# Splitting the contraction of a graph product into two 64-row halves that sum in two PSUM banks

## The chip, the cores and the metric

The kernel runs on one core of one Trainium2 chip. The metric is the device time of one execution in microseconds (us). Lower is better. I quote the median of several executions.

## The reference, cut to what matters

Four layers of graph operations act on x of shape (8, 2048, 64). Each of the first three multiplies by the same 2048 x 2048 matrix `adj`:

```python
h = relu(layernorm(x)); x = x + L0(h, adj, ...)   # T1 = A h, T2 = A T1, then weights per node
h = relu(layernorm(x)); x = x + L1(h, adj, ...)   # three steps: v = relu([v, A v] W1' + b1) W2' + b2
h = relu(layernorm(x)); x = x + L2(h, adj, ...)   # A h, a column scale, one small matmul
h = relu(layernorm(x)); x = x + L3(h, adj, ...)   # attention; with this adj a mean over the nodes
```

The matrix is 0/1 with every row scaled, so the kernel keeps its signs in `BT` (float32r, exact) and scales the result by a row of constants, `crow`. To hold precision, every operand is split into a rounded part H and a rest L, both float32r, and both are multiplied.

## The kernel before

Two of the eight batches go together as 128 feature columns. A product is 16 chunks of 128 nodes, each with H and L, so 32 matmuls of 128 rows and 512 columns, which all add into one PSUM bank. There are 88 calls of it: 24 in layer 0, 48 in layer 1 and 16 in layer 2. `fill` puts other work between chunks.

```python
def product(hl, nb, name, out, crow, fill={}):
    ps = bank("mm", f"bv_{name}")                       # one bank, two in rotation
    for m in range(NCH):                                # 16 chunks
        for i in range(2):                              # H, L
            nc.tensor.matmul(ps, hl[m // 4][i][:, m % 4, :], BT[:, m, nb * 512:(nb + 1) * 512],
                             start=(m == 0 and i == 0), stop=(m == NCH - 1 and i == 1))
        if m in fill:
            fill[m]()
    return scaled(ps, out, crow)                        # VectorE: out = ps * crow

def back_to_nodes(fT, wmat, name, tag="big"):           # "bn": four 128-row fp32 matmuls
    ps = psums[-1].tile([P, 4, 2 * C], F32, tag=tag, name=f"bn_{name}")
    ...

# layer 0, weights per node: y, 64-row fp32 matmuls, one half of the rows for each batch
y = psums[-1].tile([P, 2, 512], F32, tag="big", ...)    # a pair of banks, two pairs in rotation
for k in range(K):
    for bb in range(2):
        hs_ = slice(bb * C, (bb + 1) * C)
        nc.tensor.matmul(y[:, bb, :], terms[k][hs_, ts], wt[hs_, k, ...], ...)

# layer 1, one step of three (cut)
for nb in range(NB):
    ph = bank("tr", f"ph_{nm}")
    fill = {8: mid} if nb == 3 else {}                  # mid: bn of quarter 2
    fill[12] = lambda: nc.tensor.matmul(ph, w1v2 if s else w1vT, gT[nb], start=True, stop=True)
    product(hl, nb, nm, g, crow, fill=fill)
    gadd = nc.vector.tensor_tensor(g, ph, g, op=ALU.add)
    nc.scalar.activation(g, g, AF.Relu, bias=...)
    if nb in (1, 2):
        finish(nb - 1)                                  # bn of g, add, H and L for the next step
...
finish(3)
```

ph, bn, pt (transposes) and pS (sums over nodes) use all 128 rows. The order in which each engine runs its instructions is fixed when the program is built, and it need not be the order of this text.

Of the kernel before, what the change touches and what calls it, by code (L numbers as in the profile page):

```python
# [8 lines left out]
F32 = mybir.dt.float32  # L9
# [5 lines left out]
ALU = mybir.AluOpType  # L15
# [27 lines left out]
def uniform_path(  # L43
# [30 lines left out]
    nc = tc.nc  # L74
    P = 128
    B, N, C = x.shape
    NP = B // 2
    NCH = N // P
# [7 lines left out]
    psums = [pro.enter_context(tc.tile_pool(name="psump", bufs=1, space=bass.MemoryType.PSUM))]  # L86
# [5 lines left out]
    BT = adjp.tile([P, NCH, N], F32R, name="BT")  # L92
# [8 lines left out]
    def bank(tag, name):  # L101
        return psums[-1].tile([P, 512], F32, tag=tag, name=name)
# [12 lines left out]
    def part(nb):  # L115
        return slice(4 * nb, 4 * nb + 4)

    def load_x(layer, p, nb, queue=nc.sync):
        acc = block("acc", f"acc_{layer}_{p}_{nb}", 2)
        fill_x(acc, layer, p, nb, queue)  # L120
        return acc
# [12 lines left out]
    def load_h(p, nb, name, pool):  # L134
        t = pool.tile([P, 4, 2 * C], F32, tag="hb", name=f"hb_{name}", bufs=2)
        (nc.sync if lastp else nc.scalar).dma_start(t, hs[p][:, part(nb), :])
        return t

    def load_crow(nb, name, tag="crow"):
        t = work.tile([P, 512], F32, tag=tag, name=f"crow_{name}", bufs=2)  # L140
        nc.sync.dma_start(t, crowD[:, nb * 512:(nb + 1) * 512].to_broadcast([P, 512]))
        return t
# [41 lines left out]
    def go_on():  # L184

        with tc.issue_after(ahead.pop().ins) if ahead else nullcontext():
            for e in list(pending):
                next(e[0])
                e[1] -= 1
                if e[1] == 0:  # L190
                    pending.remove(e)
        ahead.clear()
# [8 lines left out]
    def halves(src, name, pool=None, later=None):  # L201

        pool, bufs = (work, 6) if pool is None else (pool, 4)
        Hq = pool.tile([P, 4, 2 * C], F32R, tag="H", name=f"H_{name}", bufs=bufs)
        Lq = pool.tile([P, 4, 2 * C], F32R, tag="L", name=f"L_{name}", bufs=bufs)
        copies.append(nc.scalar.copy(Hq, src))  # L206
        def rest():
            lows.append(nc.vector.tensor_tensor(Lq, src, Hq.bitcast(F32), op=ALU.subtract))

        rest() if later is None else later.append(rest)  # L210
        return Hq, Lq

    def scaled(ps, out, crow):
        ahead.append(nc.vector.tensor_tensor(out, ps, crow, op=ALU.mult))  # L214
        return out

    def product(hl, nb, name, out, crow, fill={}):

        ps = bank("mm", f"bv_{name}")
        for m in range(NCH):  # L220
            for i in range(2):
                nc.tensor.matmul(  # L222
                    ps, hl[m // 4][i][:, m % 4, :], BT[:, m, nb * 512:(nb + 1) * 512],
                    start=(m == 0 and i == 0), stop=(m == NCH - 1 and i == 1),
                )
            if m in fill:
                fill[m]()
        return scaled(ps, out, crow)

    def transposed(src, name):  # L230

# [5 lines left out]
    def to_feat(h, out, name):  # L237
        pt = transposed(lambda t: h[:, t, :], name)
        nc.scalar.copy(out, pt.rearrange("p t n -> p (t n)"))
        return out  # L240
# [41 lines left out]
    def spare(tag, name):  # L282
        return work.tile([P, 512], F32, tag=tag, name=name, bufs=6)
# [5 lines left out]
    dg = [spare("HL"[q % 2], f"dg_{q}").rearrange("p (j n) -> p j n", j=4) for q in range(NB)]  # L289
# [197 lines left out]
    nm = "0_1_3a"  # L487
    tx = work.tile([P, 512], F32, tag="z", name=f"t1T_{nm}", bufs=3)
    ps = bank("b1", f"bv_{nm}")
    for m in range(NCH):  # L490
        if m in (2, 7, 12):
            go_back(1 + m // 5)
        for i in range(2):
            nc.tensor.matmul(
                ps, hls[1][m // 4][i][:, m % 4, :], BT[:, m, 3 * 512:],
                start=(m == 0 and i == 0), stop=(m == NCH - 1 and i == 1),
# [77 lines left out]
    w1e = consts.tile([P, P], F32, name="w1e")  # L574
    ivt = consts.tile([1, P], F32, name="ivt")

    def feat(i, name):

        if i == 0:
            return term(1, name)  # L580
        return lastp[0].tile([P, 512], F32, tag="fm", name=name, bufs=4)

    def back_to_nodes(fT, wmat, name, tag="big"):

        ps = psums[-1].tile([P, 4, 2 * C], F32, tag=tag, name=f"bn_{name}")
        for t in range(4):
            nc.tensor.matmul(ps[:, t, :], fT[:, t * P:(t + 1) * P], wmat, start=True, stop=True)  # L587
        return ps
# [5 lines left out]
    def prepare_next(n, q):  # L594
        if n >= len(items):
            return
        layer, p = items[n]
        nm = f"{layer}_{p}_{q}"
        hl, gT = ops.setdefault(n, ([], []))
        h = load_h(p, q, nm, lastp[0] if n else l0q)  # L600
        if layer == 1:
            if q == 0:
                nc.scalar.copy(h[0:1, 0, :], ivt)
            gT.append(to_feat(h, feat(0, f"gT_{nm}"), nm))
            h = back_to_nodes(gT[q], w1e, f"u_{nm}", "big" if n else "mm")
        hl.append(halves(h, nm))

    def keep(p, nb, acc, name, more=None):

        norm_relu(acc, name, lambda z: nc.gpsimd.dma_start(hs[p][:, part(nb), :], z))  # L610
        if more is not None:
            nc.gpsimd.tensor_tensor(acc, acc, more, op=ALU.add)  # L612
        kept.append(nc.gpsimd.dma_start(xs[p][:, part(nb), :], acc))  # L613
# [3 lines left out]
    def node_weights(p, nb, terms, between=None):  # L617
        acc = load_x(0, p, nb)
        bn = l0q.tile([P, 4, C], F32, name="bn", bufs=2)
        nc.sync.dma_start(bn, biasD[:, part(nb), :])  # L620

        odd = l0q.tile([P, 4, 2 * C], F32, name="odd")
        av = acc.rearrange("p j (b c) -> p j b c", b=2)
        ov = odd.rearrange("p j (b c) -> p j b c", b=2)
        for t in range(4):
            ts = slice(t * P, (t + 1) * P)
            for dg in range(D // DG):
                y = psums[-1].tile([P, 2, 512], F32, tag="big", name=f"y_{p}_{nb}_{t}_{dg}")
                for k in range(K):
                    for bb in range(2):  # L630
                        hs_ = slice(bb * C, (bb + 1) * C)
                        nc.tensor.matmul(  # L632
                            y[:, bb, :], terms[k][hs_, ts], wt[hs_, k, dg * 512:(dg + 1) * 512],
                            start=(k == 0), stop=(k == K - 1),
                        )
                for d in range(DG):
                    e = dg * DG + d
                    yd, ec = y[:, :, d * C:(d + 1) * C], emb[:, 4 * nb + t, e:e + 1]
                    xj = (av, ov)[d % 2][:, t]
                    old = xj if e != 1 else bn[:, t, None, :].to_broadcast([P, 2, C])  # L640
                    last = nc.vector.scalar_tensor_tensor(  # L641
                        xj, yd, ec, old, op0=ALU.mult, op1=ALU.add
                    )
            ahead.append(last)
            chain.append(last)
            go_on()
            if between:
                between(t)
        nc.vector.tensor_tensor(acc, acc, odd, op=ALU.add)  # L649
        keep(p, nb, acc, f"1_{p}_{nb}")  # L650
# [6 lines left out]
    for p in range(NP):  # L657
# [27 lines left out]
        for nb in range(NB):  # L685
            nm = f"0_{p}_{nb}b"
            crow = load_crow(nb, nm)
            t2T = product(
                hl1, nb, nm, term(2, f"t2T_{nm}"), crow,
                fill={8: lambda: prepare(2)} if nb == 3  # L690
                else {12: lambda: first_t0.append(feat_0(0, 0))} if p + nb == 0 else {},
            )
            if p + nb == 0:
                t0T = first_t0[0]
            go_on()
            if nb == 3:
                prepare(3)
            t0T_next = feat_0(*divmod(4 * p + nb + 1, 4)) if 4 * p + nb + 1 < 4 * NP else None
            node_weights(
                p, nb, (t0T, t1T[nb], t2T),  # L700
                (lambda t: prepare_next(0, t)) if 4 * p + nb + 1 == 4 * NP else None,
            )
            t0T = t0T_next
            if nb in (1, 2):
                prepare(nb - 1)
            with tc.issue_after(kept[-1].ins):
                m = 4 * p + nb
                nc.gpsimd.dma_start(MD[m * P:(m + 1) * P, :], BTf[:, m, :])
            if p == 0:
                reload_t1(nb)  # L710
                norm_0(2, nb)
        if p == 0:
            hl1, t1T = hl_next, t1T_next
        else:
            hl = hl_next
# [56 lines left out]
    def layer1(n, p):  # L772
        hl, gT = ops[n]
        steps = 3
        for s in range(steps):
# [16 lines left out]
            def mid():  # L792
                if last:
                    prepare_next(n + 1, 2)
                else:
                    finish(2)
# [715 lines left out]
```

## Time and profile before

| before | value |
|---|---|
| time, median | 1279.28 us |
| span of the profiled execution | 1278.6 us |
| busy: TensorE, VectorE, ScalarE, GpSimd | 95%, 59%, 14%, 19% |
| first y to first ph (layer 0) | 553.5 us |
| first ph to first result of layer 2 (layer 1) | 458.0 us |
| from there to the end | 162.5 us |

TensorE is the bound. Its busy share says less than it seems to, since the recorded durations of pipelined matmuls overlap. In the views, PE is TensorE, PEld its weight loads, DVE VectorE, ACT ScalarE, POOL GpSimd and SP SyncE; L222 is line 222 of the kernel.

### The profile page before, as it was taken

To read this page: it belongs to the slowest core of one execution; us is meant where nothing else is said; L and a number is where in the kernel's file an instruction comes from. 1 tells how busy PE (TensorE), PEld (TensorE's weight loads), DVE (VectorE), ACT (ScalarE), POOL (GpSimd) and SP (SyncE) were. 2 spreads that over 40 slices of the span, in tenths; PEclk is the share of its full clock that TensorE was granted. 3 is DMA by queue.
4 is the path that set the end of the run, shared out by engine and by line. 5 is a ranking of instruction groups with operands and counts; after the bars stand their busy time and mean duration, and the time that the engine had idled before them with its cause. 6 is when DMAs were issued, how large, how long until landed. Compare 5 with 4: busy or idle time off the path is not lost.

```text
span 1278.6 us, 15515 instructions
## 1 busy us (share of the span) xinstructions
PE 1217.3 (95%) x5702; PEld 862.7 (67%) x5702; DVE 751.4 (59%) x1936; ACT 182.3 (14%) x281; POOL 236.8 (19%) x244
## 2 busy tenths in 40 slices
PE   4899999999999999999999999999999999999993
PEld 3665554555575556755567888787788787788882
DVE  5445887767746776377654446445543554575653
ACT  5530010000010000000011121112111111211100
POOL 6410211111121111011110024004102400432222
PEclk9999999999999999999999999999999999999996
DMA  8982343323332222122255425433643543524321
GB/s 265 343 208 74 96 112 87 90 70 84 95 105 71 71 79 66 65 62 62 67 141 136 102 93 158 112 92 121 150 117 87 159 116 86 161 95 115 108 58 36
DMA packets 140057, 141.14 MB, mean 110 GB/s; under 512 B 95093, under 2 KB 97141, under 8 KB 137925
## 3 DMA queue, kind: packets, MB, share of 16 engines
q1 hardware_dynamic: 121092, 82.05, 25.2%
q0 software_dynamic: 12160, 49.10, 12.8%
q10 hardware_dynamic: 6720, 8.92, 2.5%
q8 instruction: 47, 0.77, 0.2%
q14 instruction: 38, 0.30, 0.1%
HBM read 95.92 MB, written 35.73 MB: 103 GB/s over the span
## 4 chain that ended last, share of the span: by engine, by line
PE 83%; DMA 6%; DVE 4%; issue 3%; POOL 2%; ACT 1%; SPq 0%; ACTq 0%; POOLq 0%; DVEq 0%
PE bv L222 34%; PE y L632 23%; PE bn L587 4%; PE ph L804 3%; PE bv_0b L222 2%; PE bv_2b L222 2%; DMA BT<-in_adj_dram 2%; PE bv_3b L222 2%; PE bv_1b L222 2%; DMA hb<-hs 1%; POOL rstd L170 1%; PE bv_0a L222 1%; PE bv_3a L222 1%; PE bv_2a L222 1%; PE bv_1a L222 1%
## 5 line engine op out<-in xcount | busy, mean ns | idle before, releaser
L222 PE MATMUL bv<-BT,H 128*128 128x512 f32 x1024 | 426.7, 417 | 0.0
L222 PE MATMUL bv<-BT,L 128*128 128x512 f32 x1024 | 401.2, 392 | 0.0
L222 PEld LDWEIGHTS bv<-BT,H 128*128 128x128 f32 x1024 | 192.6, 188 | 47.9 <-issue 11.6
L222 PEld LDWEIGHTS bv<-BT,L 128*128 128x128 f32 x1024 | 192.9, 188 | 47.3 <-issue 11.5
L641 DVE SCALAR_TENSOR_TENSOR acc<-y,emb,acc 128x128 f32<-128x128 f32 x512 | 176.2, 344 | 65.8 <-PE y L632 62.4
L632 PE MATMUL y<-wt,t0T 64*128 64x512 f32 x512 | 144.2, 608 | 10.0 <-DVE odd L641 10.0
L641 DVE SCALAR_TENSOR_TENSOR odd<-y,emb,odd 128x128 f32<-128x128 f32 x448 | 153.3, 342 | 0.0
L170 POOL TENSOR_TENSOR rstd<-var,mhalf 128x8 f32<-128x8 f32 x64 | 107.9, 1688 | 194.5 <-DVE var L168 184.3
L214 DVE TENSOR_TENSOR g<-bv,crow 128x512 f32<-128x512 f32 x48 | 33.2, 691 | 183.7 <-PE bv L222 183.7
L164 ACT ACTIVATE sq<-z 128x512 f32<-128x512 f32 x64 | 40.4, 631 | 406.5 <-DVE z L160 397.4
L632 PEld LDWEIGHTS y<-wt,t0T 64*128 64x128 f32 x512 | 46.7, 187 | 73.9 <-issue 68.0
L612 POOL TENSOR_TENSOR acc<-acc,wl 128x512 f32<-128x512 f32 x16 | 20.6, 1289 | 297.3 <-DVE z L160 297.2
L613 POOL DMA_DIRECT2D xs<-acc x32 | 18.0, 562 | 276.2 <-DVE acc L649 254.2
L632 PE MATMUL y<-wt,t1T 64*128 64x512 f32 x256 | 67.9, 596 | 0.0
L173 DVE SCALAR_TENSOR_TENSOR z<-z,rstd 128x512 f32<-128x512 f32 x64 | 45.9, 723 | 28.2 <-POOL rstd L170 28.2
L587 PEld LDWEIGHTS bn<-wl,g 128*128 128x128 f32 x384 | 49.5, 191 | 6.3 <-ACT H L206 1.6
L167 DVE TENSOR_REDUCE var<-sq 128x8 f32<-128x512 f32 x64 | 43.5, 679 | 15.8 <-ACT sq L164 15.8
L587 PE MATMUL bn<-wl,g 128*128 128x128 f32 x384 | 51.1, 276 | 1.0 <-DVE var L168 0.5
L749 DVE SCALAR_TENSOR_TENSOR junk<-mt,cols,st 128x512 uint8<-128x512 bf16 x64 | 50.8, 794 | 0.6
L632 PEld LDWEIGHTS y<-wt,t1T 64*128 64x128 f32 x256 | 27.7, 188 | 27.3 <-issue 27.3
L809 ACT ACTIVATE g<-g,b1s 128x512 f32<-128x512 f32 x32 | 23.2, 724 | 139.4 <-DVE g L808 139.3
L160 DVE TENSOR_TENSOR z<-acc,mean 128x512 f32<-128x512 f32 x56 | 38.3, 690 | 6.6 <-DMA hs<-z 5.2
(209 smaller groups left out, 1677.3 us busy)
## 6 DMA issues: line engine op xcount, KB each, us to landing
BT<-in_adj_dram POOLq DMA_DIRECT2D x16, 1024.0 KB, 9.2
crow<-crowD SPq DMA_DIRECT2D x64, 256.0 KB, 3.2
st<-in_adj_dram SPq DMA_DIRECT2D x64, 256.0 KB, 3.4
hs<-z POOLq DMA_DIRECT2D x40, 256.0 KB, 2.8
xs<-acc POOLq DMA_DIRECT2D x32, 256.0 KB, 2.5
MD<-BT POOLq DMA_DIRECT2D x16, 512.0 KB, 5.0
acc<-xs SPq DMA_DIRECT2D x32, 256.0 KB, 3.2
hb<-hs SPq DMA_DIRECT2D x28, 256.0 KB, 3.6
```

The lines of the kernel that those rows point to most:

```text
L160: firsts.append(nc.vector.tensor_tensor(g, groups(xt), mean[:, :, None].to_broadcast([P, 8, C]), op=ALU.subtract))
L164: squares.append(nc.scalar.activation(sq, z, AF.Square))
L167: nc.vector.tensor_reduce(var, groups(sq), axis=AX.X, op=ALU.add)
L170: powers.append(nc.gpsimd.tensor_tensor(rstd, var, mhalf, op=ALU.pow))
L173: nc.vector.scalar_tensor_tensor(groups(h), g, 0.0, rstd[:, :, None].to_broadcast([P, 8, C]), op0=ALU.max, op1=ALU.mult)
L214: ahead.append(nc.vector.tensor_tensor(out, ps, crow, op=ALU.mult))
L222: nc.tensor.matmul(ps, hl[m // 4][i][:, m % 4, :], BT[:, m, nb * 512:(nb + 1) * 512], start=(m == 0 and i == 0), stop=(m == NCH - 1 and i ...
L587: nc.tensor.matmul(ps[:, t, :], fT[:, t * P:(t + 1) * P], wmat, start=True, stop=True)
L632: nc.tensor.matmul(y[:, bb, :], terms[k][hs_, ts], wt[hs_, k, dg * 512:(dg + 1) * 512], start=(k == 0), stop=(k == K - 1),)
L641: last = nc.vector.scalar_tensor_tensor(xj, yd, ec, old, op0=ALU.mult, op1=ALU.add)
L749: nc.vector.scalar_tensor_tensor(junk, mt, cols[:, i, :], st, op0=ALU.mult, op1=ALU.not_equal, accum_out=bad[:, i, q:q + 1],)
L804: fill[12] = lambda: nc.tensor.matmul(ph, w1v2 if s else w1vT, gT[nb], start=True, stop=True)
```

## The change

The intent is to let the two halves of the array work on the two halves of a chunk at the same time, so that the loading of weights for one half hides behind the other. Each half sums in a bank of its own, so a product now has two banks of sums, which ScalarE (a copy) and VectorE (an add) join. For the banks, y and the products share three pairs, and bn moves to the two "tr" banks.

```diff
     def product(hl, nb, name, out, crow, fill={}):
-        ps = bank("mm", f"bv_{name}")
+        ps = psums[-1].tile([P, 2, 512], F32, tag="big", name=f"bv_{name}", bufs=3)
         for m in range(NCH):
             for i in range(2):
-                nc.tensor.matmul(
-                    ps, hl[m // 4][i][:, m % 4, :], BT[:, m, nb * 512:(nb + 1) * 512],
-                    start=(m == 0 and i == 0), stop=(m == NCH - 1 and i == 1),
-                )
+                for r in range(2):
+                    rows = slice(r * C, (r + 1) * C)
+                    nc.tensor.matmul(
+                        ps[:, r, :], hl[m // 4][i][rows, m % 4, :],
+                        BT[rows, m, nb * 512:(nb + 1) * 512],
+                        start=(m == 0 and i == 0), stop=(m == NCH - 1 and i == 1),
+                    )
             if m in fill:
                 fill[m]()
-        return scaled(ps, out, crow)
+        nc.scalar.copy(out, ps[:, 1, :])
+        nc.vector.tensor_tensor(out, ps[:, 0, :], out, op=ALU.add)
+        return scaled(out, out, crow)
 ...
-    def back_to_nodes(fT, wmat, name, tag="big"):
-        ps = psums[-1].tile([P, 4, 2 * C], F32, tag=tag, name=f"bn_{name}")
+    def back_to_nodes(fT, wmat, name):
+        ps = psums[-1].tile([P, 4, 2 * C], F32, tag="tr", name=f"bn_{name}")
 ...
-                y = psums[-1].tile([P, 2, 512], F32, tag="big", name=...)
+                y = psums[-1].tile([P, 2, 512], F32, tag="big", name=..., bufs=3)
```

More of the change, by code (lines that the diff above doesn't have):

```diff
@@ L604, in prepare_next @@
             gT.append(to_feat(h, feat(0, f"gT_{nm}"), nm))
-            h = back_to_nodes(gT[q], w1e, f"u_{nm}", "big" if n else "mm")
+            h = back_to_nodes(gT[q], w1e, f"u_{nm}")
         hl.append(halves(h, nm))
@@ L627, in node_weights @@
             for dg in range(D // DG):
-                y = psums[-1].tile([P, 2, 512], F32, tag="big", name=f"y_{p}_{nb}_{t}_{dg}")
+                y = psums[-1].tile([P, 2, 512], F32, tag="big", name=f"y_{p}_{nb}_{t}_{dg}", bufs=3)
                 for k in range(K):
```

## The prediction

> **What bounds the kernel now.** I read the page's chain of work first, then busy times by stage, then the instructions of single stretches in order of time, because a pipelined TensorE looks busy whatever it does. The chain that ended last, by engine and by line:
>
> ```profile
> PE 83%; DMA 6%; DVE 4%; issue 3%; POOL 2%; ACT 1%; SPq 0%; ACTq 0%; POOLq 0%; DVEq 0%
> ```
>
> The rest of that part gives `bv L222`, the line that the change rewrites, 34% under its plain name and more under bv_0b to bv_3a. By stage (the loading, layer 0 in two stretches, layer 1, layer 2):
>
> ```profile
> 100.00:385.00 285.00, 276.68 (x1265) 162.47 (x1263) 204.73 (x648) 23.50 (x39) 43.77 (x47) 0.99 0.34 87
> 652.00:1108.00 456.00, 455.00 (x2169) 365.54 (x2169) 221.85 (x419) 79.22 (x129) 78.89 (x73) 1.00 0.47 122
> 1108.00:1279.00 171.00, 145.88 (x766) 124.34 (x764) 99.09 (x177) 18.52 (x32) 46.53 (x33) 0.94 0.32 92
> ```
>
> The columns are length, then busy us of PE, PEld, DVE, ACT and POOL. PE is full in layer 1 (455 of 456), and DVE is at 222, ACT at 79. So only TensorE's own time counts from 100 us on, and 2816 product matmuls (88 calls of 32) hold most of it. Their recorded 0.39 us is not their cost. The cost is the distance between starts, in order of time in layer 1:
>
> ```profile
> 700.03 0.39 PE L222 MATMUL bv<-BT,L 128*128 128x512 f32 x1
> 700.26 0.39 PE L222 MATMUL bv<-BT,H 128*128 128x512 f32 x1
> ...
> 701.62 0.39 PE L222 MATMUL bv<-BT,H 128*128 128x512 f32 x1
> 701.84 0.39 PE L222 MATMUL bv<-BT,L 128*128 128x512 f32 x1
> ```
>
> Eight steps take 1.81 us, 226 ns each. Over all 2485 such steps inside runs of L222 the median is 227 and the mean 228.7 ns. So the products cost 2816 x 228.7 = 644 us, half of the kernel, and there are no gaps in them that a wait would explain.
>
> **What the Trainium skill says.** "TensorE: Matmul & The Clock Gate", section Back-to-back issue gap, gives N / 2.4 + 2.5 ns for a warm matmul, 215.8 ns at 512 columns. These take 227, so 11 ns of each are above that floor; they are all the change can win. The same page, Part 3, The mechanism, says that matmuls in different row groups run concurrently. The trace agrees for the 64-row matmuls of y (below). It also says that weight loads overlap running matmuls only when the row group differs. The trace contradicts this: a load for the same 128 rows starts at 700.26, with the matmul before it, and lasts 0.19 us of the 0.227. No weight loading is left in the open for halves to hide. "TensorEngine Tiling (Array Packing)", section Tiling Modes, Key Properties, says that changing the tiling mode drains TensorE. The trace agrees, and this decides my prediction. "PSUM — Partial Sum Buffer", Specifications (TRN2), allows a VectorE instruction one tensor input from PSUM, hence the join by a ScalarE copy and then an add.
>
> **The change, part by part.**
>
> *The halves.* Each product gets 64 matmuls for 32, in pairs on rows 0-63 and 64-127. Each half still streams 512 columns, so a pair that runs side by side costs what one full matmul costs, at best the floor. What the pair will cost I take from fp32, where both forms exist. The y matmuls come in fours in 0.859 us (310.10, 310.96 below), 0.429 us a pair. The 128-row ph matmul with as many columns (L804) goes from 702.52 to 702.95, 0.43 us. So there pairing gives what the full array gives, no more. By this analogy I put a pair at 226 ns, with 216 as the best case. Gain: 2816 x (228.7 - 226) = 8 us; at 216, 36 us.
>
> *The changes of mode.* Today TensorE changes between 64 and 128 rows only around y. Entering the products from y:
>
> ```profile
> 310.10 1.05 PE L632 MATMUL y<-wt,t1T 64*128 64x512 f32 x4
> 310.96 1.05 PE L632 MATMUL y<-wt,t2T_2b 64*128 64x512 f32 x4
> 311.94 0.50 PE L222 MATMUL bv_3b<-BT,H_t 128*128 128x512 f32 x1
> 312.28 0.40 PE L222 MATMUL bv_3b<-BT,L_t 128*128 128x512 f32 x1
> ```
>
> 312.28 - 310.96 = 1.32, less 0.859 for the four and 0.227 for one product matmul: 0.24 us lost. The other way, transposes to y:
>
> ```profile
> 319.38 0.60 PE L234 MATMUL pt<-ident,hb_f 128*128 128x128 f32 x4
> 319.91 1.13 PE L632 MATMUL y<-wt,t0T 64*128 64x512 f32 x4
> 320.87 1.02 PE L632 MATMUL y<-wt,t1T 64*128 64x512 f32 x4
> ```
>
> 320.87 - 319.38 = 1.49, less 4 x 0.107 and 0.859: 0.20 us lost. (All 13 of the first kind have a median of 0.241, all 18 of the second 0.199.) Between works that both use 128 rows nothing is lost:
>
> ```profile
> 704.54 0.40 PE L222 MATMUL bv<-BT,L 128*128 128x512 f32 x1
> 704.77 1.06 PE L587 MATMUL bn<-wl,g 128*128 128x128 f32 x8
> 705.59 0.48 PE L222 MATMUL bv<-BT,H 128*128 128x512 f32 x1
> 705.90 0.39 PE L222 MATMUL bv<-BT,L 128*128 128x512 f32 x1
> ```
>
> 705.90 - 704.54 = 1.36, less two of 0.227 and 8 x 0.1095: 0.03 us for the way there and back. After the change the products are 64-row work and bn, ph, pt and pS stay 128-row work, and they sit in the middle of the products: layer 1 interrupts each product for ph and again for bn. I counted, in the order of the trace before, the borders at which the mode would differ: 175 each way, 110 of them in layer 1, 30 in layer 2, 35 in layer 0, against 22 each way now, all in layer 0. The change adds 153 round trips of 0.437 us: 67 us on the engine that sets the end.
>
> *The joining.* One ScalarE copy (like L206's casts from PSUM, 580 ns) and two VectorE operations in place of one (like L214's, 691 ns):
>
> ```profile
> L214 DVE TENSOR_TENSOR g<-bv,crow 128x512 f32<-128x512 f32 x48 | 33.2, 691 | 183.7 <-PE bv L222 183.7
> L206 ACT CAST H<-bn 128x512 fp32r<-128x512 f32 x32 | 18.6, 580 | 49.5 <-DVE bn L789 49.5
> L632 PE MATMUL y<-wt,t0T 64*128 64x512 f32 x512 | 144.2, 608 | 10.0 <-DVE odd L641 10.0
> ```
>
> DVE gets 88 x 0.69 = 61 us, ACT 88 x 0.58 = 51 us, spread over engines that are half idle: beside other work. What reaches the path is the result's delay, 0.58 + 0.69 + about 0.1 of signals = 1.4 us later. In layer 1 the next step needs its last quarter only at chunk 12, 24 steps of 0.227 = 5.4 us after its start, plus the interruptions, so it is hidden, though barely. In layer 0, y needs the sum at its third term: after pt and two terms, some 0.6 + 0.2 + 1.7 = 2.5 us, against 0.58 + 0.69 + 0.69 + 0.3 = 2.3 us. I charge 5 us for the 16 blocks when something else sits in front, and 2 us for the kernel's tail.
>
> *The banks.* y gets a third pair of banks, which can take back some of the 10.0 us that PE waited for DVE in the last row (7 times): -4 us. bn moves to the two "tr" banks and shares them with ph, pt and pS, which is a chance of new waits; I charge none in the centre.
>
> Sum: 1279.1 - 8 + 67 + 5 + 2 - 4 = 1341 us.
>
> **Rivals.** (1) *The pair reaches the floor of 216 ns.* For it: fp32 matmuls come within 3 ns of their floor (429 against 2 x 213.3), so the 11 ns belong to this type and might go with smaller loads. Against: each half still reads 512 columns in its own rows at the same rate. Then 36 us come back instead of 8: 1313 us. Fewer borders, if the order of instructions is built differently, make 1300. (2) *The pair costs more than one full matmul,* because TensorE must take four instructions in 227 ns. For it: y needs four per 429 ns only, and the densest runs here (bn, 8 matmuls with 8 loads in 0.88 us) are short. At 240 ns: 40 us more than at 226, 1381 us. If such halves did not overlap at all, 2816 x 227 = 640 us would be added, near 1950; y's overlap speaks against it, but y streams at half this rate. (3) *The two "tr" banks become the bound:* ph is held until its add, which now comes 1.4 us later. With one wait of 0.5 us for each of the 48 + 16 products of the last two layers, 32 us: 1373. Against: bn is read within some 2 us. (4) *The change wins over 2%:* it would need the floor and almost no cost of the mode; no view supports it.
>
> **Range and chances.** The switching cost is measured tightly (67 us, perhaps 50 to 75 if the order shifts). The pair's cost is the widest term, 216 to 240, so -36 to +32 us; new waits add 0 to 30. I take 1308 to 1385 as 8 in 10. Within 2% means under 1304.7 us, which only rival 1 with fewer borders gives: 0.08. Faster by over 2%: 0.03. Slower: 0.89.
>
> **What would show it.** In the profile after, starts of pairs within layer 1 should be about 226 ns apart, both halves starting within some 40 ns; far less or more decides rivals 1 and 2. Each border between bv and bn, ph, pt or pS should lose 0.2 to 0.24 us where it lost under 0.02, and layer 1 should grow from 456 by about 45 us, layer 0 by under 15. The stretch up to 90 us should not move. DVE should be some 61 us busier and PE should still hold the chain. I am wrong if the borders lose nothing, if pairs are not side by side, or if PE waits for banks.

## The result, and the profile after

The changed kernel takes 1366.52 us (1365.21 to 1368.28, 4 runs), against 1279.28 us before. The ratio is 1.067, with a 95% interval of 1.063 to 1.071. Ratios here are the mean time of one kernel's fast runs over the mean of the other's fast runs of the same rounds, so they are not quite the ratio of the medians that I quote. The changed kernel is 87 us slower. The prediction was 1341 us, 62 us slower, with a range of 1308 to 1385.

The chain that ended last in the changed kernel, by engine:

```profile
PE 83%; DVE 6%; DMA 5%; ACT 2%; issue 1%; POOL 1%; SPq 1%; ACTq 0%; POOLq 0%; DVEq 0%
```

TensorE still carries it with the same share of a longer span. Busy times by stage say where the span grew. The stretches go from the first y to the first ph, to the first result of layer 2, to the end. The columns are length, then busy us of PE, PEld, DVE, ACT and POOL, clock, DMA. First before, then after:

```profile
104.60:658.10 553.50, 540.79 (x2466) 316.63 (x2466) 386.50 (x1239) 40.68 (x68) 72.66 (x83) 0.99 0.30 78
658.10:1116.10 458.00, 456.45 (x2173) 366.39 (x2171) 221.38 (x418) 78.64 (x128) 80.88 (x74) 1.00 0.47 124
1116.10:1278.60 162.50, 138.33 (x732) 118.41 (x732) 96.17 (x171) 17.89 (x31) 41.75 (x29) 0.94 0.30 84
```

```profile
104.10:660.00 555.90, 541.07 (x3228) 321.48 (x3227) 402.23 (x1261) 53.81 (x92) 72.23 (x83) 0.99 0.30 78
660.00:1186.80 526.80, 508.34 (x3707) 362.48 (x3707) 249.29 (x465) 108.66 (x176) 82.55 (x76) 0.99 0.42 108
1186.80:1363.90 177.10, 152.13 (x1225) 120.12 (x1221) 105.69 (x186) 27.04 (x47) 40.88 (x27) 0.94 0.27 76
```

Layer 0 grew by 2.4 us, layer 1 by 68.8 and the rest by 14.6. The clock is the same within 0.01. Next, the products themselves, in order of time in layer 1 of the changed kernel:

```profile
763.09 0.40 PE L228 MATMUL bv<-BT,H 64*128 64x512 f32 x2
763.32 0.40 PE L228 MATMUL bv<-BT,L 64*128 64x512 f32 x2
...
764.00 0.40 PE L228 MATMUL bv<-BT,H 64*128 64x512 f32 x2
```

Each line is a pair ("x2"). Pairs follow each other at 0.227 us, as single full matmuls did before. The halves of a pair start 3 ns apart in the median. So they do run side by side, and it gains nothing: over all whole pairs inside runs the mean step is 229.7 ns, against 228.7 for the full matmuls. The full matmuls left no weight loading in the open to hide (the prediction shows a load beginning with the matmul before and lasting 0.19 us of the 0.227). That the 512 columns set the step is the reading that fits; no run varied them.

Next, the border between the products and bn in the changed kernel:

```profile
755.58 0.40 PE L228 MATMUL bv<-BT,L 64*128 64x512 f32 x2
755.91 1.16 PE L596 MATMUL bn<-wl,g 128*128 128x128 f32 x8
757.00 0.50 PE L228 MATMUL bv<-BT,H 64*128 64x512 f32 x2
757.33 0.40 PE L228 MATMUL bv<-BT,L 64*128 64x512 f32 x2
```

757.33 - 755.58 is 1.75 us. Less two pairs of 0.227 and 8 x 0.1095 for bn, 0.42 us are lost, where the same border lost 0.03 us before.

Some borders lose more. This is the last bn of a step of layer 1, with VectorE and ScalarE shown too:

```profile
868.81 0.39 PE L228 MATMUL bv<-BT,H 64*128 64x512 f32 x1
869.26 0.69 DVE L817 TENSOR_TENSOR g<-ph,g 128x512 f32<-128x512 f32 x1
...
869.99 0.72 ACT L818 ACTIVATE g<-g,b1s 128x512 f32<-128x512 f32 x1 [2.21 <-DVE g L817]
...
870.76 1.16 PE L596 MATMUL bn<-wl,g 128*128 128x128 f32 x8 [1.57 <-ACT g L818]
```

TensorE has one half of a pair to do at 868.81 (the other half comes after bn) and then waits for ScalarE's relu until 870.76. This border loses 2.06 us, counting that half as free, which is 1.86 us more than a border without a wait, and there are 8 of them: 15 us of waiting. In the kernel before, 11 full matmuls of the next product stood in front of this bn, 2.5 us of work. Here 17 halves do, 8.5 pairs, 1.9 us, while the result now passes through a copy and one more VectorE operation before it gets there: the next product starts at 866.99 and the relu ends at 870.71, 3.7 us later.

The groups that answer to the joining, from the changed kernel's page (the copy, the add, and y's waits):

```profile
L235 ACT COPY g<-bv 128x512 f32<-128x512 f32 x48 | 28.1, 586 | 213.3 <-PE bv L228 213.2
L236 DVE TENSOR_TENSOR g<-bv,g 128x512 f32<-128x512 f32 x48 | 33.2, 692 | 223.9 <-ACT g L235 223.9
L641 PE MATMUL y<-wt,t0T 64*128 64x512 f32 x512 | 139.7, 599 | 0.6 <-DVE odd L650 0.6
```

Both durations are as expected (586 and 692 ns). TensorE's idle time before y fell from 10.0 to 0.6 us.

I went through all matmuls in order of time, took each at its steady cost (0.227, 0.4293, 0.1095 us and so on) and assigned the rest to the border where it stood. Counting 0.2 us of a border with a wait as change of mode, this gives (borders of products or y with bn, ph, pt and pS; four borders at single small matmuls are in the rest):

| where | before, us | after, us | difference |
|---|---|---|---|
| changes of mode (43 before, 363 after) | 9 | 74 | +65 |
| waits at borders | 9 | 36 | +27 |
| inside y, waits for VectorE and banks | 17 | 3 | -14 |
| products, 2816 steps of 228.7 or 229.7 ns | 644 | 647 | +3 |
| the rest | | | +4 |

The differences add up to 85 us, which is the growth of the profiled span (1278.6 to 1363.9); "the rest" is what closes the sum. One wait of 4.8 us belongs there: a single matmul, pf, waits for VectorE at 1177 us, at the end of layer 1.

### The profile page after: what moved, and what is told of

It is laid out like the page before. It is cut to its first block, busy times and chain, and to the rows that moved or that the text cites.

```text
span 1363.9 us, 21342 instructions
## 1 busy us (share of the span) xinstructions
PE 1283.3 (94%) x8518; PEld 864.9 (63%) x8518; DVE 804.7 (59%) x2024; ACT 235.0 (17%) x369; POOL 237.2 (17%) x244
## 4 chain that ended last, share of the span: by engine, by line
PE 83%; DVE 6%; DMA 5%; ACT 2%; issue 1%; POOL 1%; SPq 1%; ACTq 0%; POOLq 0%; DVEq 0%
PE bv L228 33%; PE y L641 24%; PE bn L596 5%; PE ph L813 3%; PE bv_2b L228 2%; PE bv_0b L228 2%; PE bv_1b L228 2%; DMA BT<-in_adj_dram 2%; PE pt L243 1%; PE bn_u L596 1%; PE bv_2a L228 1%; PE pS L862 1%; PE bv_3b L228 1%; PE bv_3a L228 1%; DMA hb_f<-hs 1%
## 5 line engine op out<-in xcount | busy, mean ns | idle before, releaser
L228 PE MATMUL bv<-BT,H 64*128 64x512 f32 x2048 | 430.5, 404 | 0.0
L228 PE MATMUL bv<-BT,L 64*128 64x512 f32 x2048 | 419.3, 393 | 0.0
L228 PEld LDWEIGHTS bv<-BT,H 64*128 64x128 f32 x2048 | 216.3, 186 | 83.6 <-issue 36.9
L228 PEld LDWEIGHTS bv<-BT,L 64*128 64x128 f32 x2048 | 217.3, 186 | 39.8 <-issue 1.5
L236 DVE TENSOR_TENSOR g<-bv,g 128x512 f32<-128x512 f32 x48 | 33.2, 692 | 223.9 <-ACT g L235 223.9
L641 PE MATMUL y<-wt,t0T 64*128 64x512 f32 x512 | 139.7, 599 | 0.6 <-DVE odd L650 0.6
L641 PEld LDWEIGHTS y<-wt,t0T 64*128 64x128 f32 x512 | 50.3, 187 | 55.6 <-issue 52.9
L596 PE MATMUL bn<-wl,g 128*128 128x128 f32 x384 | 55.6, 288 | 13.0 <-ACT g L818 13.0
L235 ACT COPY g<-bv 128x512 f32<-128x512 f32 x48 | 28.1, 586 | 213.3 <-PE bv L228 213.2
L158 DVE TENSOR_REDUCE mean<-acc 128x8 f32<-128x512 f32 x56 | 37.9, 683 | 9.6 <-DMA acc<-in_x_dram 8.4
```

The costliest lines, as they stand in the source:

```text
L158: nc.vector.tensor_reduce(mean, groups(xt), axis=AX.X, op=ALU.add)
L228: nc.tensor.matmul(ps[:, r, :], hl[m // 4][i][rows, m % 4, :], BT[rows, m, nb * 512:(nb + 1) * 512], start=(m == 0 and i == 0), stop=(m == ...
L236: nc.vector.tensor_tensor(out, ps[:, 0, :], out, op=ALU.add)
L596: nc.tensor.matmul(ps[:, t, :], fT[:, t * P:(t + 1) * P], wmat, start=True, stop=True)
```

## The experiments

The theory is that the changes of mode cost 65 us, that waits which the instruction order does not cover cost most of the rest, and that the joining and the banks cost little by themselves. Rivals are that the joining is the cost, that the shared "tr" banks are, that the borders' loss is only a wait read wrongly, and that halves lose wherever they stand. All these kernels gave correct results. The kernel before ran beside them with medians of 1281.22, 1280.07 and 1281.05 us in the three batches.

### Full rows, with the joining kept (first batch)

```diff
-                for r in range(2):
-                    rows = slice(r * C, (r + 1) * C)
-                    nc.tensor.matmul(ps[:, r, :], hl[m // 4][i][rows, m % 4, :], BT[rows, m, ...],
-                        start=(m == 0 and i == 0), stop=(m == NCH - 1 and i == 1))
+                nc.tensor.matmul(ps[:, i, :], hl[m // 4][i][:, m % 4, :], BT[:, m, ...],
+                    start=(m == 0), stop=(m == NCH - 1))
```

> The changed kernel with its halves undone: every product matmul has 128 rows again, those of H sum in one bank and those of L in the other, and the ScalarE copy, the VectorE add and the banks stay as changed. Theory (changes of mode cost most of the loss): the some 320 added borders between 64-row and 128-row work go, at 0.2 us each that is 65 us; 1366 - 65 = 1301 us, and the waits of bn for ScalarE's relu stay (8 of about 2 us in layer 1). Rival (the longer joining and the shared banks cost most): it stays above 1340 us.

Measured: 1271.17 us, ratio 0.993 (0.991 to 0.995). It is 95 us faster than the changed kernel, although it has the same copy, add and banks. So the joining and the banks are not the cost; the halves are. It went 30 us below what I expected, because the waits went too: those of layer 1 just shown, about 15 us, and about 13 us in layer 0 (see the halves in layer 0 below). For layer 1 the trace tells why. The last bn of a step here stands behind 17 matmuls of the next product:

```profile
676.30 0.72 ACT L816 ACTIVATE g<-g,b1c 128x512 f32<-128x512 f32 x1 [2.21 <-DVE g L815]
...
676.94 0.39 PE L226 MATMUL bv<-BT,H 128*128 128x512 f32 x1
...
677.17 1.07 PE L594 MATMUL bn<-wl,g 128*128 128x128 f32 x8
```

The relu ends at 677.02, and bn follows the matmul before it at 0.23 us: nothing is lost. The joining is just as long here; it is covered by 17 x 0.229 = 3.9 us of the next product instead of 1.9. This made the order of the instructions a suspect of its own.

### The banks alone (first batch, and again with more rounds)

This is the kernel before with the changed banks: full rows into one bank of a pair, no joining.

```diff
-        ps = bank("mm", f"bv_{name}")
+        ps = psums[-1].tile([P, 2, 512], F32, tag="big", name=f"bv_{name}", bufs=3)   # sums in ps[:, 0, :]
...  # bn in "tr", y with bufs=3, as in the change
```

> The kernel before with the changed banks only: products with 128 rows into one bank and no join, three pairs of banks for y and the products, bn in the two tr banks. Theory: the third pair takes away y's waits, which the trace of the changed kernel shows as 14 us less inside the y stretches; the tr banks cost nothing; 1279 - 14 = 1265 us. Rival (the tr banks are the source of the new waits, some 30 us): 1295 us or more.

Measured: 1265.67 us, ratio 0.990 (0.987 to 0.993). That is the expected time. In its trace y loses 3.6 us (2.6 of them in the first block), against 17 us before. The kernel beats both, so I repeated it with five rounds:

> The banks-only kernel once more, with more rounds, to settle whether it beats the kernel before by more than noise: the first time gave 0.990 (0.987 to 0.993). Theory (y's waits of 17 us go, some of it is given back elsewhere): 0.988 to 0.992 again. Rival (the first run was a lucky stretch): 0.995 or more.

Measured: 1264.40 us, ratio 0.988 (0.986 to 0.990). The gain is confirmed. It is the only part of the change that pays.

### bn in the "tr" banks alone (second batch)

```diff
-        ps = psums[-1].tile([P, 4, 2 * C], F32, tag=tag, name=f"bn_{name}")
+        ps = psums[-1].tile([P, 4, 2 * C], F32, tag="tr", name=f"bn_{name}")
```

> The kernel before with one thing changed: bn in the two tr banks; y keeps two pairs of banks and the products their two single banks. Theory (the third pair of banks for y is what makes the banks-only kernel faster): y's waits stay and the time is 1279 us, within 5. Rival (bn's leaving the pairs frees them for y): near 1266 us.

Measured: 1278.40 us, ratio 0.999 (0.998 to 1.001). So moving bn neither costs nor gains, and the gain of the banks-only kernel comes with the three pairs that y and the products rotate through.

### One small matmul more in each product, with 64 rows or with 128 (first batch)

This was added to the banks-only kernel:

```diff
+            if m == 6:                                  # rows: 0:64 in one kernel, 0:128 in the other
+                nc.tensor.matmul(ps[:, 1, :C], hl[0][0][rows, 0, :], BT[rows, 0, :C], start=True, stop=True)
```

> The banks-only kernel with one small 64-row matmul (64 columns, into the unused bank) after chunk 6 of each of the 88 products, result unused. Theory: each brings two changes of mode, 0.44 us, and its own 0.03 to 0.1 us: 88 x 0.5 = 44 us over the banks-only kernel, some 38 us over the same matmul with 128 rows. Rival (a border costs nothing by itself and what was read there was the waiting for y's data and banks): within 5 us of the 128-row one.

> The control to the 64-row one: the same small matmul at the same place with 128 rows, the order of all instructions the same. Theory and rival alike: 88 x 0.03 to 0.1 us over the banks-only kernel, 3 to 9 us.

Measured: 1304.14 us (ratio 1.019) with 64 rows and 1280.82 us (1.000) with 128. The instruction order of the two kernels is the same on every engine, so these 23.3 us are the rows alone, 0.265 us for each of 88 visits. One visit in the trace, with 64 rows and then with 128:

```profile
716.75 0.39 PE L226 MATMUL bv<-BT,L 128*128 128x512 f32 x1
717.07 0.29 PE L232 MATMUL bv<-BT,H 64*128 64x64 f32 x1
717.29 0.50 PE L226 MATMUL bv<-BT,H 128*128 128x512 f32 x1
717.63 0.39 PE L226 MATMUL bv<-BT,L 128*128 128x512 f32 x1
```

```profile
710.15 0.39 PE L226 MATMUL bv<-BT,L 128*128 128x512 f32 x1
710.37 0.19 PE L232 MATMUL bv<-BT,H 128*128 128x64 f32 x1
710.40 0.48 PE L226 MATMUL bv<-BT,H 128*128 128x512 f32 x1
710.72 0.39 PE L226 MATMUL bv<-BT,L 128*128 128x512 f32 x1
```

From the first line to the last it is 0.88 us with 64 rows and 0.57 with 128: 0.31 us more for going to the other mode and back. Nothing waits for data there, and the result is read by nobody. So the change of mode costs by itself. I had expected some 38 us between the two; the real borders of the changed kernel lose 0.2 us each, where these lose about 0.13 to 0.16 (half of 0.265 and of 0.31; all 88 visits of each trace are within 0.02 us of the two shown). So this pair accounts for 42 to 50 of the 65 us at 160 more ways there and back. Why the real borders lose more was not tested. The small matmul itself took 0.12 us and not 0.03 to 0.1, so its control is 15 us over the banks-only kernel and not 3 to 9; in its trace there are also waits for loads in layer 0, 7.1 us in three (2.0 us in one in the banks-only kernel).

### The last bn of a step held back (second batch)

The changed kernel, with `finish(3)` of the first two steps called from the next step's first product:

```diff
-                finish(3)
+                def late(finish=finish):
+                    with tc.issue_after(at[0].ins):     # behind the second half of chunk 10
+                        finish(3)
+                held.append(late)
...
+                if nb == 0 and held:
+                    fill[10] = held.pop()
```

> The changed kernel with one thing moved: the last bn of the first two steps of layer 1 is held back to chunk 10 of the next step's first product (22 pairs in, where it now stands 14.5 pairs in). Theory (the order of the instructions puts this bn too early for the longer joining, and TensorE waits 2.06 us each of 8 times for ScalarE's relu): those waits go, and the pairs that were split there are whole again; 1366 - 16 - 2 = 1348 us. Rival (the joining itself is too long for the step): the wait only moves to chunk 12, and the time stays above 1360 us.

Measured: 1350.38 us, ratio 1.056 (1.053 to 1.059), 16 us under the changed kernel. (The "14.5 pairs" of the expectation were counted from ph. Six of those pairs still finish the product that is ending, so bn stood 8.5 pairs into the next one; here it stands 22 pairs in, 5.0 us.) The waits of 2.06 us are gone from its trace, with as many changes of mode as before and the same joining. So these 16 us were the place of one instruction group: with the joining as long as before, that work in front of bn was enough. (By the ratios the gain is 14.5 us.)

### Fewer borders (second batch), and the same with the visit later (third batch)

On top of the last kernel, ph is multiplied in the same visit as bn, so that products are interrupted 32 times less:

```diff
-                fill[12] = lambda: nc.tensor.matmul(ph, ...)
+                def visit(...):                          # bn of quarter nb - 2 (or the one held back), then ph
+                    ...
+                fill[10 if nb == 0 else 2] = visit       # the second kernel: 4 in place of 2
```

> The same and ph placed next to bn, so that one visit of 128-row work serves both: 32 visits fewer, 64 changes of mode fewer, no instruction less. Theory (0.2 us a change): 13 us under the kernel with bn held back, about 1335 us. Rival (borders do not count by themselves): within 3 us of it.

Measured: 1361.56 us, ratio 1.064, 11 us slower than without it. A miss. The waits of TensorE in this kernel (total us, times, longest us) show a new one:

```profile
PE ph L826 <- DVE g L831: 11.0, 18, 2.2
```

The time lost at borders within layer 1 did fall, from 53.1 to 40.8 us, but ph now comes so early that both "tr" banks are still taken: one by bn, and one by the ph before, whose add by VectorE is not done. Inside the visits 16.4 us are lost. So the shared banks, harmless in the kernel as changed, became a wait as soon as the order was pressed. The second kernel moves the visit by two chunks:

> The kernel with fewer borders, its joint visit of bn and ph moved from chunk 2 to chunk 4 of the product. The run before it lost 16 us inside the visits, where ph waited for VectorE's add of the ph before (11.0 us recorded, 18 times), because both tr banks were taken. Theory: at chunk 4 that add is done, the waits go, and the 64 changes of mode saved show: 13 us under the kernel with bn held back, 1337 us. Rival (fewer borders save nothing): 1350 us.

Measured: 1343.56 us, ratio 1.050 (1.047 to 1.053). Of ph's waits one is left, 1.1 us. The kernel is 7 us under the one with bn held back, about half of the 13 expected: in the traces the borders of layer 1 lose 12.6 us less (40.5 against 53.1), but the steps inside its products lose 3.3 us more and the wait of ph takes 1.1, which leaves 8 us, about what was measured. (The two profiled runs differ by 13.2 us, but 4.7 of that lies before the first y, a stretch that varies from run to run.) The direction is that of the theory, since the rival said 1350.

### Halves in layer 0 alone (second batch), and with the loads from another queue (third batch)

```diff
             for i in range(2):
+                if lastp:                                # layers 1 and 2
+                    nc.tensor.matmul(ps[:, 0, :], hl[m // 4][i][:, m % 4, :], BT[:, m, ...], ...)
+                else:
                     for r in range(2): ...
+        if lastp:
+            return scaled(ps[:, 0, :], out, crow)
```

> Halves and joining in layer 0's 24 products alone, full rows and no joining in layers 1 and 2, the changed banks throughout. Theory: next to y, which has 64 rows too, halves add only some 25 borders, 5 us, and the pair costs what a full matmul costs; with the waits that the changed kernel shows in layer 0, up to 14 us: 1271 to 1285 us, so most of the loss is layer 1's and 2's. Rival (halves lose by themselves, wherever they are): a share of 24 of 88 of the 95 us that the joined full-row kernel is faster, 26 us over the banks-only kernel, 1292 us.

Measured: 1286.00 us, ratio 1.005 (1.003 to 1.006), 20 us over the banks-only kernel, 1 us above what I expected (1271 to 1285) and 6 below the rival, so it does not decide between them by itself. By the trace the pairs there also follow each other at 0.227 us, and 22 more borders make 4 us; about 13 us are waits that the banks-only kernel and the joined full-row kernel do not have. The longest are the same as in the changed kernel, where TensorE's waits read:

```profile
PE pt L243 <- DMA hb_f<-hs: 5.6, 2, 2.8
...
PE pt_t L243 <- DVE t1T_0a L214: 4.2, 1, 4.2
```

I suspected that the loads of hb_f (h, read back from memory to be transposed for y) come late because ScalarE, which issues them, is held up by its copies:

```diff
-        (nc.sync if lastp else nc.scalar).dma_start(t, hs[p][:, part(nb), :])
+        nc.sync.dma_start(t, hs[p][:, part(nb), :])
```

> Halves in layer 0 alone, and the loads of hb and hb_f issued from SyncE's queue instead of ScalarE's. Theory (two of the waits in layer 0, 3.0 and 3.2 us, are loads of hb_f that ScalarE issues late, behind its copies, in the order that the kernel got): those two waits go, 6 us under the 1286 us, 1280 us. Rival (the loads wait for their buffer, whoever issues them): unchanged, 1286 us.

Measured: 1289.83 us, ratio 1.007, not better. My reason fell and the rival holds: in the changed kernel the load is issued at 308.49 us, right after VectorE has read the last of the two buffers (until 308.45), and from SyncE's queue one is issued at 308.31, again right after such a read (until 308.28). A third buffer does not fit; the build refuses it, since the pool would need 10 kB a partition where 8.2 are left. What makes VectorE and ScalarE come to these buffers later than in the joined full-row kernel, which does the same work, I did not settle. The order of instructions on these engines differs between the two, but that this is the cause is only argued. Halves are not needed for such waits: the control with one small 128-row matmul has neither halves nor joining, and waits 7.1 us for hb_f.

## Why the prediction was right or wrong

The prediction was right in direction and range, and its main mechanism held: halving gains nothing, and going back and forth between 64 and 128 rows costs. Its centre was 25 us too low. The misses partly cancel: the banks gained 10 us more than foreseen, while the pairs cost 11 and the waits 20 more. Without the banks' surplus the time would have been some 1377 us, still in the range, so the range did not need that luck. By its steps:

- *The halves* (-8 us predicted). Whole pairs take 229.7 ns a step in the mean, against 228.7 before: +3 us. The argument from fp32, that a pair costs what a full matmul costs, was right, and the small gain that I added to it was not. Rival 1 (216 ns) and rival 2 (240 ns, or no overlap) fell in the trace.
- *The changes of mode* (67 us predicted, 153 round trips). The trace has 320 more borders, 160 ways there and back of 0.41 us, and loses 65 us more at them. The joined full-row kernel shows that this goes with the halves, and the pair of small matmuls that 0.27 to 0.31 of the 0.41 us come from the rows alone; the kernel with fewer borders lost 12.6 us less for 64 changes of mode less. Layer 1 grew by 68.8 us where about 45 were foreseen: the changes of mode there are as foreseen (237 of about 0.2 us, 47 us), and the waits for the relu (15) and of pf (4.8) come on top.
- *The joining* (5 + 2 us charged to waits). This is the step that failed, in size and in the place of the wait. I wrote that in layer 1 the delay "is hidden, though barely", counting with 24 steps to chunk 12. But TensorE does not wait for the next step's data first; it waits at bn, whose place among the matmuls was set when the program was built, 8.5 pairs into the next product. Waits at borders grew by 27 us. Holding bn back regained 16 us of the total. With full rows the same joining cost some 5 us in all (1271.17 against 1265.67, which is hardly clear of noise: the intervals of the two ratios overlap). VectorE is 53.3 us busier by the page, not 61. No run tests what the prediction cites for the need of the joining, that VectorE takes one input from PSUM.
- *The banks* (-4 us). The third pair took away 14 us inside y, not 4. I read only the 10.0 us of idle time on one row of the page; the steps inside y's stretches sum to 17 us. Rival 3 (the "tr" banks) did not come true in the changed kernel, as the kernel with bn moved alone shows (0.999), but it did in the kernel with the early visits.

## What to carry to other kernels

Before splitting rows, measure the steps of the full matmul. Here they already hid their weight loads, pairs of halves followed at the same 0.227 us, and every border with full-row work then cost 0.2 us. After changing the shape of the instructions, look at where the build has put the work that waits for results, because a longer path to a result is free only while enough work stands in front of it. And try the parts of a change one by one: here the banks alone gain 1.2%, and the rest of the change hides that.

## What the Trainium skill lacked or had wrong

- "TensorEngine Tiling (Array Packing)", Tiling Modes, Key Properties: it says that a change of the tiling mode drains TensorE, but gives no cost. In the kernel before it is 0.20 us from 128 to 64 rows and 0.24 us from y back to the products; in the changed kernel about 0.2 us each way; and 0.31 us for both ways around a single small matmul. The loss fits a drain, but the traces show only the later starts.
- "TensorE: Matmul & The Clock Gate", Part 3, The mechanism: weight loads are said to overlap running matmuls only where the row group differs (the same section also speaks of a background weight buffer, which would fit better). Here loads for the same 128 rows start with the matmul before and are over in 0.19 us of its 0.227. The two halves of a pair start 3 ns apart, which agrees with its figure of about 4 ns.
- The same page, Back-to-back issue gap: its formula, given there for an isolated matmul, makes 215.8 ns for 512 columns. float32r matmuls follow at 227 ns, with 128 rows and in 64-row pairs alike, so the 11 ns above it are not a matter of the rows. No page has a figure for float32r.
